# Layer 0's expert lists in four waves instead of five, with the recording planner's ranks drawn anew

## The chip, the core and the metric

The kernel runs on one core of a Trainium2 chip. The metric is device microseconds per execution, the median of several. The kernel before has a median of 1212.02 us over 3 runs (1209.06 to 1213.38). The profiler took one execution by itself; that one is longer, and the text keeps it apart.

## The reference, cut to what matters

Two layers of attention and a mixture of experts, each followed by a residual add and a layer norm, all in float32, on 16 sequences of 256 tokens with 128 features:

```python
x = _layernorm(x + _L0_attn_ref(x, ...))   # RMS norm, 16 heads of 64, softmax over 256 keys
x = _layernorm(x + _L0_ffn_ref(x, ...))    # top 2 of 8 experts (hidden 256) + one shared expert
x = _layernorm(x + _L1_attn_ref(x, ...))   # per token: 16 heads attend to each other, 8 wide
x = _layernorm(x + _L1_ffn_ref(x, ...))    # top 2 of 8 experts (hidden 512)
```

The reference computes every expert for every token and masks; the kernel computes, for most tokens, only the two chosen experts.

## The kernel before, in words

**Groups and units.** The 4096 tokens are eight groups of 512 (`xg[0]` to `xg[7]`), each of four chunks of 128 rows. Layer 0's attention (`attention0`, L666) goes through 128 units, one for a group, a pair of heads and a sequence of 256: scores on PE (TensorE, L574), a maximum on DVE (VectorE, L537), exponentials on ACT (ScalarE, L543), a division on POOL (GpSimd, L558), transposes (L591) and the product with the values (L612) on PE, the latter two three units behind the scores (`LAG`). Sixteen units make a group; then `project` (L629) or `project2` (L649) gives the group's output.

**Lists and waves.** The experts' work is done in waves (`WAVES`, L33). A wave takes some groups; `route` (L799) finds each token's two experts on DVE and gives every pair of token and expert a row in a list that is sorted by expert and padded to tiles of 128 rows. With c chunks in a wave the list has 2c + 7 tiles (`NTS`), enough for any split over eight experts. `send` (L896) copies the tokens' rows into the list in HBM with indirect DMAs that POOL issues, two for each chunk (L905). `lists` (L969) loads the list's rows back, four tiles at a time (L1014), and for each tile the weights of its expert (L1035 and L1039 in layer 0, L1039 and L1048 in layer 1); PE transposes the rows (L1060), does the first products (L1098) and the second ones (L1118), with GELU on ACT between them (L1077, L1071). The results go back to HBM (L1136). `gathered` (L920) fetches them with indirect DMAs from POOL, two for each chunk (L934), and DVE adds them to `x` (L948). `shared` (L1153) is layer 0's shared expert.

**What follows a wave of layer 0.** `middle` (L1397) takes each of its groups through the norm, through layer 1's attention (`attention1`, L1313; `chunk1`, L1201, one for each chunk: products on DVE and POOL at L1216 and L1292, sums on DVE at L1220 and L1267 or on PE at L1226 and L1274) and to the logits of layer 1's router. Layer 1 has three waves of its own, groups 0 to 3, groups 4 and 5, groups 6 and 7; a wave of layer 1 begins when all its groups have their logits (`wave1`, L1411).

**The dense part.** The second sequence of group 7 goes through all experts without lists (`sequence`, L1569, and `dense`, L1502; its products at L1528 and L1541).

**What sets the order.** Nothing is reordered at run time. The kernel's parts are generators ("strands"); while the program is recorded, `everything` (L322) picks the strand to go on with by a small planner: each strand says when its next step can start by the planner's own clocks, `KEYS` gives each kind of strand a rank and a lead in time, `PACE` gives attention0 a lead for each half group, and `COPY`, `SUMS`, `FAVOUR`, `SWITCH` bias which engine a copy or a product goes to. What comes out is one fixed sequence for each engine, and each engine works its own sequence in order and waits at its head. A new value in `WAVES`, `KEYS` or `PACE` therefore moves thousands of instructions without changing what most of them do.

Only one list is open at a time (`held` has "lists"); in layer 1 a list that is not the last can be interrupted by one of layer 0 or by the last one. The names used below: "list 0_3" is layer 0's wave 3, "list 1_0" layer 1's wave 0, and so on.

Of the kernel before, what the change touches and what calls it, by code (L numbers as in the profile page):

```python
# [29 lines left out]


PARTS = [(g, 0, NC) for g in range(LAST)] + [(LAST, 0, NC // 2)]
WAVES = (((0,), (1,), (2, 3), (4, 5), (6, 7)), ((0, 1, 2, 3), (4, 5), (6, 7)))  # L33
I32 = mybir.dt.int32


# [1 line left out]
def two_layers(  # L38
# [81 lines left out]

    CS = [[sum(PARTS[i][2] for i in w) for w in ws] for ws in WAVES]
    NTS = [[2 * c + 7 for c in cs] for cs in CS]
# [14 lines left out]
    def cleared(layer, w):  # L137
# [10 lines left out]

    INF = float("inf")
    KEYS = {  # L150
        "copy qk": (-0.126, 0.098),
        "copy v": (0.258, 0.464),
        "copy p": (0.365, 0.67),
        "copy o": (-2, 0.171),
        "softmax": (-0.332, 0.347),
        "softmax 2": (-0.557, 0.071),
        "summed": (-1.741, 0.444),
        "normalised": (0.126, 0.737),
        "heads": (-0.897, 0.036),
        "w route": (0.203, 0.017),  # L160
        "w send": (-0.299, 0.32),
        "w shared": (-0.925, 0.219),
        "w loads": (-0.335, 0.546),
        "w turns 0": (-0.74, 0.23),
        "w turns 1": (-0.883, 0.07),
        "w firsts 0": (-0.387, 0.019),
        "w firsts 1": (1.618, 0.545),
        "w gelu": (-0.526, 0.095),
        "w seconds 0": (-0.551, 0.301),
        "w seconds 1": (1.137, -0.645),  # L170
        "w stored": (-1.046, -0.735),
        "w gathered 0": (0.929, 0.295),
        "w gathered 1": (0.397, -0.379),
        "w qkv": (-1.874, 0.602),
        "w attention1": (0.552, 0.037),
        "w attention1 2": (0.862, 0.362),
        "w sums": (0.545, 0.099),
        "w normed": (-0.751, 0.178),
        "d loads": (-1.222, 0.561),
        "d route": (0.341, 0.516),  # L180
        "d firsts": (-0.612, -0.163),
        "d gelu": (0.532, 0.418),
        "d seconds": (-0.409, -0.744),
        "d added": (-0.448, 0.337),
        "d normed": (-0.4, 1.013),
    }
    PACE = [-1.37, 1.462, -1.273, -1.636, 1.503, -0.385, -0.54, 1.281]
    PACE += [1.979, 0.872, 0.936, -0.178, 0.47, 1.169, 0.679, 1.086]
    now = [0]
    COPY = -0.06  # L190
    SUMS = 7.789
    FAVOUR = 0.378
    SWITCH, SWITCH_BACK = 0.582, 1.515
    window, unit = [0, 0.0, 1.0], [P]
    clk = {"PE": 0.0, "DVE": 0.0, "ACT": 0.0, "POOL": 0.0, "SP": 0.0}
    table = ["exp"]
# [65 lines left out]
    def copied(o, i, *after):  # L262
# [5 lines left out]
        dve, act = (max(clk[e], *after) + t for e, t in zip(EITHER, us))  # L268
        if dve + COPY <= act:
            nc.vector.tensor_copy(o, i)  # L270
# [37 lines left out]
    def key(what, w=0, i=0):  # L308

        rank, time = KEYS[what]  # L310
        return (time, rank, w, i)
# [5 lines left out]
    def begin(steps, key):  # L317
        st = Strand(steps, key)
        if st.due is not None:
            strands.append(st)  # L320
# [13 lines left out]

    DENSE = len(WAVES[0])
    held = []
# [100 lines left out]
    def after(*names):  # L437

        return lambda: max(end.get(n, INF) for n in names)
# [27 lines left out]
    def normalised(g):  # L467
# [10 lines left out]
        yield at, EITHER  # L478
        if max(clk["DVE"], at) + 1.2 + COPY <= max(clk["ACT"], at) + 1.4:
            for c in range(NC):  # L480
# [16 lines left out]
        hT[g] = sb.tile([P, GT], FP, tag="hT", name=f"hT{g}")  # L497
        if max(clk["DVE"], at) + 0.75 + COPY <= max(clk["ACT"], at) + 0.7:
            nc.vector.tensor_scalar(hT[g], t, nscale_s, None, ALU.mult)
# [6 lines left out]
    def projected(g, p, w, name, to):  # L506

        yield after(("h", g), "wq"), "PE", "m"
        pq = ps_m.tile([P, GT], FP, tag="m", name=f"p{name}{g}_{p}")
        nc.tensor.matmul(pq, w[:, ts(p, P)], hT[g], start=True, stop=True)  # L510
        to[g, p] = sb.tile([P, GT], FP, tag=f"{name}T", name=f"{name}T{g}_{p}")
        begin(copy_out(opened("m"), to[g, p], pq, work("PE", 0.91), name, g, p), key("copy qk"))
# [153 lines left out]
    def attention0():  # L666
        yield from projected(0, 0, wq_s, "q", qT)
        yield from projected(0, 0, wk_s, "k", kT)
        clears = [(0, 0), (0, 1), (0, 2), (1, 0), (0, 3), (1, 1), (0, 4), (1, 2)]
        for u in range(len(UNITS) + LAG):  # L670
            if u >= LAG:
                yield from turn(u - LAG)
            g, p, b = UNITS[u] if u < len(UNITS) else (NG, 0, 0)
            i = u % (2 * NP)
            if g < NG:
                now[0] = 2 * g + i // NP
                running[-1].key = (KEYS["heads"][1], PACE[now[0]], 0, 0)
                if i == 3 and g + 1 < NG:
                    begin(normalised(g + 1), key("normalised"))
                if u + 1 < len(UNITS):  # L680
                    to = UNITS[u + 1]
                    if to[0] == LAST:
                        yield from projected2(*to[1:])
                    elif b:
                        yield from projected(*to[:2], wk_s, "k", kT)
                if g < LAST and b == 0:
                    to = (g, p + 1) if p + 1 < NP else (g + 1, 0)
                    if to[0] < LAST:
                        yield from projected(*to, wq_s, "q", qT)
                if g < LAST:  # L690
                    if i in (3, 5, 7, 9):
                        yield from values(g, 1, (i - 3) // 2)
                elif i in (1, 3):
                    yield from values(g, 1, (i - 1) // 2)
                elif i in (5, 7):
                    yield from values(g, 0, 2 + (i - 5) // 2)
                elif i in (8, 10):
                    yield from values(g, 1, 2 + (i - 8) // 2)
                if i in (11, 13, 15) and g + 1 < LAST:
                    yield from values(g + 1, 0, (i - 11) // 2)  # L700
                if i in (11, 13) and g + 1 == LAST:
                    yield from values(g + 1, 0, (i - 11) // 2)
                if i == 1 and 0 < g < LAST:
                    yield from values(g, 0, 3)
                yield from scores(u)
                if u < 2:
                    for c in (2 * u, 2 * u + 1):
                        yield from values(0, 0, c)
            if u >= LAG:
                yield from attended(u - LAG)  # L710
            if g < NG:
                if u % 3 == 2 and clears and "prepared" in end:
                    cleared(*clears.pop(0))
                if g == LAST and i == NP + LAG:
                    yield from project2(0)
                if g < LAST and i == NP + LAG:
                    yield from project(g, 0)
                if i == LAG and g > 0:
                    yield from project(g - 1, 1)
        yield from project2(1)  # L720
        end["over"] = 0.0
        now[0] = 2 * NG
# [165 lines left out]
    def chunks_of(r):  # L888
        return [(g, c0 + c) for g, c0, n in (PARTS[i] for i in WAVES[r.layer][r.wave]) for c in range(n)]

    def place_of(r, part):

        ws = WAVES[r.layer][r.wave]
        return sum(PARTS[i][2] for i in ws[: ws.index(part)])
# [74 lines left out]
    def lists(r):  # L969
# [3 lines left out]

        yields = layer == 1 and w < len(WAVES[1]) - 1
        if not yields:
# [225 lines left out]
    def chunk1(w, c, o, qv, kv, at, sums):  # L1201
# [5 lines left out]
        for j in range(2):  # L1207
            yield (lambda: max(at, prod_ring.free(), sc_ring.free() if j == 0 else 0.0)), "DVE"
            if j == 0:
                sc1, ks = sc_ring.tile([P, NH1, NH1], "sc")  # L1210
                if "over" in end and clk["PE"] + SUMS < max(clk["DVE"], at) and ends["s"][-2] < clk["PE"] + 1.0:
                    ps = ps_s.tile([P, NH1, NH1], FP, tag="s", name="s1")
# [29 lines left out]
        if place is None:  # L1242
            yield at, ("POOL", "DVE")
            e, us = ("POOL", 0.6) if max(clk["POOL"], at) <= max(clk["DVE"], at) + FAVOUR else ("DVE", 0.4)
            (nc.gpsimd if e == "POOL" else nc.vector).tensor_tensor(
# [39 lines left out]
        for j in range(2):  # L1285
            yield (lambda: max(at, prod_ring.free())), ("POOL", "DVE")
            e, us = "POOL", 2.35
            if max(clk["DVE"], at) + 1.25 + FAVOUR < max(clk["POOL"], at) + 2.35:
                e, us = "DVE", 1.25
# [8 lines left out]
            at2 = work("POOL", us, at, one=us) if e == "POOL" else work("DVE", us, at, ports=True)  # L1298
            if j == 0 and "over" in end and clk["PE"] + SUMS < max(clk["DVE"], at) and ends["s"][-2] < clk["PE"] + 1.0:
                po = ps_s.tile([P, P], FP, tag="s", name="o1_sums")  # L1300
# [65 lines left out]
    def wave(w):  # L1366

        parts, C = WAVES[0][w], CS[0][w]
        yield after("prepared"), None
# [108 lines left out]
    w = DENSE  # L1478
# [185 lines left out]
```

## Time and profile before

| what | value |
|---|---|
| median of 3 runs | 1212.02 us |
| the profiled execution's own time | 1245.39 us |
| its span on the core | 1243.7 us |
| mean granted TensorE clock | 0.943 |
| PE, DVE, ACT, POOL busy | 1109.0, 900.2, 706.0, 705.7 us |
| last `po` of layer 0's attention (L612) begins | 841.4 us |
| first transpose of list 1_0, of list 1_1, of list 1_2 (L1060) | 936, 1075, 1157 us |
| last second product of list 1_2 (L1118) ends | 1211 us |

The page's times are those of the profiled execution. In what follows the stretch up to 841 us is the head and the rest the tail. The five lists of layer 0 stand so in it: sends at 166 to 183, 214 to 227, 451 to 484, 651 to 683 and 839 to 857 us, the last of these at the start of the tail; their gathers at 231 to 242, 281 to 359, 577 to 622, 759 to 822 and 957 to 979 us. Layer 1's three lists are sent at 873 to 923, 1018 to 1038 and 1120 to 1139 us, and gathered from 1084 us to 1233 us.

How to read it: a busy PE alone doesn't say that PE is the bound. What does is a stretch in which PE has no idle time, against one in which it waits at the head of its sequence for another engine.

### The profile page before, as it was taken

What the parts mean: (1) busy time and instruction counts of PE and PEld (TensorE: products, weight loads), DVE (VectorE), ACT (ScalarE), POOL (GpSimd) and SP (SyncE); (2) the same over time, 40 slices, a digit from 0 to 9 for tenths busy, and PEclk for the clock granted to TensorE, in tenths of its full rate; (3) what the DMA queues carried; (4) which work ended last, traced back from release to release, by engine and by line L of the source; (5) the groups of instructions that cost most, each with busy time, mean ns of one, the idle gap of its engine ahead of it and who ended that gap; (6) DMA issues with size and microseconds to landing.
All of it is one profiled execution on the core that took longest, in us unless ns stands there. A gap on an engine that the chain in (4) does not pass through costs nothing.

```text
span 1243.7 us, 22712 instructions
## 1 busy us (share of the span) xinstructions
PE 1109.0 (89%) x7336; PEld 814.5 (65%) x7336; DVE 900.2 (72%) x1811; ACT 706.0 (57%) x2050; POOL 705.7 (57%) x1089
## 2 busy tenths in 40 slices
PE   9999999979999999999998899987838896797883
PEld 5566667665665666766655677655738795697883
DVE  5767675478878888754877998888878795793433
ACT  5556566476665667676674687653544552342432
POOL 4434372557555468524769557767873546446666
PEclk9999999989999999999999999987888897798997
DMA  8900023430000021151003240135458874684952
GB/s 260 270 1 1 1 86 111 132 106 14 1 5 1 1 63 58 35 145 45 18 4 100 80 133 21 29 119 164 144 162 232 257 230 129 197 245 125 288 177 70
DMA packets 187208, 132.47 MB, mean 107 GB/s; under 512 B 12745, under 2 KB 171474, under 8 KB 187090
## 3 DMA queue, kind: packets, MB, share of 16 engines
q1 hardware_dynamic: 179410, 115.27, 31.6%
q0 software_dynamic: 7680, 15.74, 4.1%
q8 instruction: 59, 0.97, 0.3%
q14 instruction: 59, 0.48, 0.1%
HBM read 97.94 MB, written 33.03 MB: 105 GB/s over the span
## 4 chain that ended last, share of the span: by engine, by line
PE 66%; DVE 11%; POOL 8%; issue 6%; ACT 4%; DMA 2%; SPq 1%; ACTq 0%; DVEq 0%; POOLq 0%
PE s L574 9%; PE po L612 9%; PE t L591 9%; PE po_e L1118 6%; PE ph L1098 6%; POOL rows L905 5%; PE py L629 4%; PE pv L528 4%; PE pq L510 4%; PE pk L510 3%; DVE qk_prod L1216 2%; DMA xq<-rows 2%; PE po_d L1541 1%; POOL pr L558 1%; DVE sc L1220 1%
## 5 line engine op out<-in xcount | busy, mean ns | idle before, releaser
L558 POOL TENSOR_SCALAR pr<-pr,rs 128x256 f32<-128x256 f32 x512 | 253.0, 511 | 220.6 <-DVE rs L554 136.7
L543 ACT ACTIVATE pr<-s,nm 128x256 f32<-128x256 f32 x512 | 235.5, 474 | 26.1 <-DVE nm L537 23.0
L537 DVE TENSOR_REDUCE nm<-s 128x4 f32<-128x1024 f32 x128 | 156.1, 1220 | 58.0 <-PE s L574 53.2
L905 POOL DMA_INDIRECT rows<-x,r_pi x120 | 130.7, 1089 | 58.6 <-DVE r_pi L853 24.4
L934 POOL DMA_INDIRECT y<-outs,r_pi x120 | 120.0, 1000 | 65.8 <-issue 27.4
L612 PE MATMUL po<-pT,v 128*64 128x256 f32 x1024 | 146.0, 397 | 7.2 <-ACT h L1077 3.1
L1098 PE MATMUL ph<-xqT,wa 128*128 128x128 f32 x1028 | 132.8, 287 | 16.6 <-issue 14.2
L591 PE MATMUL t<-ident,pr 128*128 128x128 f32 x1024 | 144.4, 283 | 0.8 <-ACT h L1077 0.8
L591 PEld LDWEIGHTS t<-ident,pr 128*128 128x128 f32 x1024 | 115.7, 145 | 42.4 <-POOL pr L558 20.6
L1098 PEld LDWEIGHTS ph<-xqT,wa 128*128 128x128 f32 x1028 | 126.9, 202 | 22.6 <-issue 16.8
L270 DVE COPY pT<-t 128x512 f32<-128x512 f32 x163 | 106.8, 686 | 42.2 <-PE t L591 38.3
L574 PEld LDWEIGHTS s<-kT,qT 64*128 64x128 f32 x896 | 77.1, 186 | 84.2 <-issue 73.1
L574 PE MATMUL s<-kT,qT 64*128 64x256 f32 x896 | 127.0, 402 | 0.0
L1292 POOL TENSOR_TENSOR av_prod<-sc,qkv 128x1024 f32<-128x1024 f32 x35 | 89.9, 2577 | 50.7 <-ACT sc L1254 35.3
L272 ACT COPY oT<-po 128x256 f32<-128x256 f32 x99 | 36.9, 373 | 130.6 <-PE po L612 119.6
L612 PEld LDWEIGHTS po<-pT,v 128*64 128x64 f32 x1024 | 65.1, 137 | 67.6 <-issue 18.9
L543 ACT ACTIVATION_READ_ACCUMULATOR pr<-s,nm 128x1 f32 x512 | 105.5, 206 | 0.0
L1118 PE MATMUL po_e<-wb,h 128*128 128x128 f32 x648 | 84.3, 292 | 5.5 <-issue 5.5
L1118 PEld LDWEIGHTS po_e<-wb,h 128*128 128x128 f32 x648 | 82.6, 209 | 5.3 <-issue 4.8
L1216 DVE TENSOR_TENSOR qk_prod<-qkv 128x1024 f32<-128x1024 f32 x64 | 82.8, 1294 | 1.8 <-ACT qkv L272 1.8
L1267 DVE TENSOR_REDUCE o<-av_prod 128x64 f32<-128x1024 f32 x62 | 73.3, 1200 | 11.3 <-POOL apart L904 9.7
L1220 DVE TENSOR_REDUCE sc<-qk_prod 128x128 f32<-128x1024 f32 x64 | 78.1, 1220 | 2.2
(233 smaller groups left out, 1971.0 us busy)
## 6 DMA issues: line engine op xcount, KB each, us to landing
wa<-in_w_dram SPq DMA_DIRECT2D x190, 128.0 KB
wa<-in_w_dram SPq DMA_DIRECT2D x81, 256.0 KB
wb<-in_w_dram SPq DMA_DIRECT2D x81, 256.0 KB
xq<-rows SPq DMA_DIRECT2D x38, 256.0 KB
outs<-yq SPq DMA_DIRECT2D x38, 256.0 KB
rows<-clear SPq DMA_DIRECT2D x3, 1472.0 KB
rows<-clear SPq DMA_DIRECT2D x1, 2496.0 KB
rows<-clear SPq DMA_DIRECT2D x2, 1216.0 KB
```

Of the source, the lines that this page charges most:

```text
L270: nc.vector.tensor_copy(o, i)
L537: nc.vector.tensor_reduce(nm[u], s, AX.X, ALU.max, negate=True)
L543: nc.scalar.activation(pr[u][:, i, :], s[:, i, :], AF.Exp, bias=nm[u][:, i : i + 1], accum_out=su[u][:, i : i + 1],)
L558: nc.gpsimd.tensor_scalar(pr[u][:, i, :], pr[u][:, i, :], rs[:, i : i + 1], 1.0, ALU.mult, ALU.mult)
L574: nc.tensor.matmul(sc[u][:, j, qc, :], q[part, ts(qc, P)], k[part, :], start=True, stop=True,)
L591: nc.tensor.transpose(t[:, kc, ts(qc, P)], pr[u][:, 2 * j + qc, ts(kc, P)], ident)
L612: nc.tensor.matmul(po[j * DH : (j + 1) * DH, :], vs[g, p // 4, 2 * b + kc][:, ts(h, DH)], pT[u][j][:, kc, :], start=(kc == 0), stop=(kc == 1),
L905: i = nc.gpsimd.indirect_dma_start(out=rows[layer][w][:, :], out_offset=bass.IndirectOffsetOnAxis(ap=r.pos[:, k, c : c + 1], axis=0), in_= ...
L934: nc.gpsimd.indirect_dma_start(out=y, out_offset=None, in_=outs[layer][w][:, :], in_offset=bass.IndirectOffsetOnAxis(ap=r.pos[:, k, c0 + c ...
L1098: nc.tensor.matmul(ph[:, q - q0, c, :], was[i, q][0][:, c, :], xTs[i][0][:, q, :], start=True, stop=True)
L1118: nc.tensor.matmul(po[:, q, :], hs[i, q][0][:, c, :], wbs[i, q][0][:, c, :], start=(c == 0), stop=(c == nh - 1))
L1216: nc.vector.tensor_tensor(m, q3[:, ts(j, HALF)].unsqueeze(2).to_broadcast(full), k3.unsqueeze(1).to_broadcast(full), ALU.mult)
```

## The change

The diff touches constants only. Its core:

```diff
-WAVES = (((0,), (1,), (2, 3), (4, 5), (6, 7)), ((0, 1, 2, 3), (4, 5), (6, 7)))
+WAVES = (((0,), (1, 2), (3, 4), (5, 6, 7)), ((0, 1, 2, 3), (4, 5), (6, 7)))
...
     KEYS = {
-        "copy qk": (-0.126, 0.098),
+        "copy qk": (-0.774, 0.185),
...
-        "w send": (-0.299, 0.32),
+        "w send": (-1.721, 0.333),
...
-    PACE = [-1.37, 1.462, -1.273, -1.636, 1.503, -0.385, -0.54, 1.281]
-    PACE += [1.979, 0.872, 0.936, -0.178, 0.47, 1.169, 0.679, 1.086]
+    PACE = [-1.701, -1.793, -0.961, -1.029, -0.823, 0.7, 1.677, 1.623]
+    PACE += [1.623, 1.362, -1.327, 0.173, 1.701, 2, 1.82, 1.503]
...
-    COPY = -0.06
-    SUMS = 7.789
-    FAVOUR = 0.378
-    SWITCH, SWITCH_BACK = 0.582, 1.515
+    COPY = 0.617
+    SUMS = 7.519
+    FAVOUR = 0.528
+    SWITCH, SWITCH_BACK = 1.21, 0.864
...
-        clears = [(0, 0), (0, 1), (0, 2), (1, 0), (0, 3), (1, 1), (0, 4), (1, 2)]
+        clears = [(0, 0), (0, 1), (0, 2), (1, 0), (0, 3), (1, 1), (1, 2)]
```

All 35 entries of `KEYS` have new values. With c = 4, 4, 8, 8, 6 chunks the lists of layer 0 had 15, 15, 23, 23 and 19 tiles, 95 in all; with c = 4, 8, 8, 10 they have 15, 23, 23 and 27, 88 in all. Group 5, which was in a wave with group 4, is now in the last one, with 6 and the first sequence of 7. One of the clears of the lists' memory goes.

Both programs can be built and their sequences compared without being run. Counts of instructions, and where they stand in each engine's sequence, are taken from there below.

## The prediction

> **What bounds the kernel now.** I read first the page's 40 slices and then the busy time by stage, cut at the points where PE's sequence passes from one kind of work to the next.
>
> ```profile
> PE   9999999979999999999998899987838896797883
> PEclk9999999989999999999999999987888897798997
> ```
>
> The first line is PE's busy tenths, the second the granted clock. But for slice 9 and slices 22 and 23, PE is full up to slice 26; behind it there are holes, and the clock sinks with them.
>
> ```profile
> core 0: us, PE busy (x) PEld busy (x) DVE busy (x) ACT busy (x) POOL busy (x), PEclk, DMA share, GB/s
> 0.00:841.00 841.00, 806.28 (x5176) 535.05 (x5176) 632.40 (x1210) 539.28 (x1727) 470.13 (x792) 0.98 0.23 68
> 841.00:936.00 95.00, 61.30 (x359) 50.00 (x359) 76.88 (x139) 42.10 (x98) 70.48 (x100) 0.81 0.53 163
> 936.00:1075.00 139.00, 110.06 (x814) 104.59 (x813) 107.29 (x196) 59.63 (x102) 66.09 (x74) 0.84 0.74 218
> 1075.00:1157.00 82.00, 71.66 (x522) 67.64 (x521) 51.29 (x136) 34.30 (x61) 43.89 (x55) 0.90 0.60 177
> 1157.00:1211.00 54.00, 47.18 (x376) 45.36 (x377) 19.69 (x80) 21.57 (x42) 35.50 (x42) 0.97 0.81 233
> 1211.00:1244.00 33.00, 12.49 (x97) 11.89 (x96) 12.66 (x55) 9.08 (x20) 19.64 (x29) 0.76 0.23 67
> ```
>
> The head is bound by PE: 806 of 841 us. The tail is not: in 403 us PE works 303. I call its stages A (to the first transpose of list 1_0), B (to that of 1_1), C (to that of 1_2), D (to the last second product) and E. In A, DVE and POOL are busier than PE. What PE waits for in A is in the timeline of PE:
>
> ```profile
> 917.00 0.38 PE L419 MATMUL t_x<-ident,o 128*128 128x128 f32 x2
> 932.58 0.69 PE L419 MATMUL t_x<-ident,o 128*128 128x128 f32 x2 [15.20 <-DVE o L1308]
> ```
>
> A transpose of layer 1's attention output stood 15.2 us at the head of PE's sequence, until DVE had finished the chunk; everything behind it stood too.
>
> **The change, part by part.** I take each instruction's time up to the start of the next on its engine, from the trace; so taken, a first product costs 0.247 us, a second 0.243, a list transpose 0.14. A tile of layer 0 (one transpose, two of each product) costs PE 1.1 us.
>
> *Seven tiles and one routing less.* 7 x 1.1 = 8 us of PE; but 16 more sums go to PE (L1226, 0.33 each, as L1274), 5 us. PE's total is nearly unchanged. Seven tiles also save 14 GELUs and 7 pairs of weight loads; one route saves about 40 short DVE instructions, scan included, some 10 us. These lie beside PE work in the head. So the tiles themselves are worth little; what counts is where the work goes.
>
> *The head gets shorter.* Its lists were 15 + 15 + 23 + 23 = 76 tiles, and are 15 + 23 + 23 = 61. Up to the last L612, PE has 30 first products, 30 second ones and 15 transposes less, 17 us; and of the shared expert, routing and layer 1's attention of one group and a half some 11.5 us less: 28.5 us. The head's PE idle time is 35 us: 11 of it lie at 205 to 300, where two waves' sends and gathers kept POOL from the divisions of L558, 8 at 650 to 705, in the sends of wave (4, 5). The new order has one wave less, but puts sends in one block: 16 in a row before unit 55's and unit 89's divisions. At the timeline's pitch of 1.27 us for a send (0.96, a memset, the gap) a block is 20 us; three units of `LAG` at 5 us (the scores of units 103 and 105 are 10 us apart) cover 15, and PE's order has 6 us of shared-expert products in the hole. Bounds: 0 to 20 us of hole for a block; the nearest row, the 16 sends at 651 to 683, cost 8. I take the idle time as unchanged, 35 us. The head ends at 841.4 - 28.5 = 813.
>
> *Copies.* `COPY` sends 104 copies more to ACT and 109 fewer to DVE. ACT's 539 us in the head rise by about 98 x 0.5 less the GELUs saved, to some 565 of 813; DVE falls by 70. PE still covers both; an exponential that waits behind one copy in ACT's sequence loses at most 0.59 us (a copy of `pT`). Bounds -10 to +10 us, taken at nothing.
>
> *The tail gets 25 us more PE work* (296 us to 321 by the same counting): 8 tiles, the shared expert for three parts, one more group of layer 1's attention, the sums. By stage, before and after: A 55.8 and 92.5; B 105.5 and 134.1; C 71.9 and 54.5; D 49.0 and 39.9; E 13.8 and 0. The dense experts' products, which lay in C, D and E, now lie in A and B (19 and 32 us). POOL's work behind its last division goes from 240 to 270 us (8 sends and 8 gathers more), DVE's behind its last maximum from 283 to 268.
>
> Stage A. List 1_0 can't start before its rows are sent. DVE passed 34.7 us of work from its last maximum (826) to the list positions (873), 47 us, 0.74; up to group 4's `y` (87.7 us, 937) it was 0.79. In the new order 56.4 us stand before those positions, because group 3's attention now ends in the tail: 74 us at 0.76, so 59 us after the head's end. Then 32 sends x 1.27 = 41, and about 10 for the rows' load: A = 110 (95 before). POOL has finished the 20 sends of 0_3 before. PE's own 92.5 fit, if it stands no more than 17 us; group 4's transpose, the one shown, comes at 65.5 us of DVE work, at about 70 us, and 35 us of PE work follow it.
>
> Stage B. List 1_0 itself: 101 us of PE plus 20 of standing (29 in B before, 10.9 in one wait for a weight load): 121. Now the sends of 1_1 stand on POOL behind six gathers of 1_0, which wait for all of 1_0's results: 3 + 6 gathers and the products between them, 9, + 16 sends, 20, + 9 for the load = 41. Dense products, 33 us, cover PE for most of it. B = 162 (139 before). 1_1's positions are due at 186.4 us of DVE work, about 225 us behind the head, and 1_0's end at 231: just hidden.
>
> Stages C, D, E. At before's ratios: 54.5 x 82/71.9 = 62; 39.9 x 54/49.0 = 44; E, the last gathers and norms on POOL and DVE, stays 33, since the dense products that go from it lay beside them. POOL has the sends of 1_2 done some 49 us of work behind those of 1_1, inside C.
>
> Sum: 813 + 110 + 162 + 62 + 44 + 33 = 1224 us of span. The profiled execution's time is 1.7 us over its span: 1225.7 against 1245.4, 0.984. Applied to the median: 1212 x 0.984 = 1193.
>
> *A rule that speaks against it.* The Trainium skill, "TensorE: Matmul & The Clock Gate", Part 1, says that PE drops to half clock after an idle window of about 3.4 us. The change moves 25 us of PE work from a head at clock 0.98 to a tail at 0.81 to 0.90. By the rule at its worst they cost 50, and the forecast 1217, slower. The trace: the 304 records of second products in the head took 37.27 us, 0.123 each; in B 312 took 41.86, 0.134, in D 152 took 18.25, 0.120. Products come in bursts that are warm; I take the row, at most 9% or 2 us, which the stages' ratios contain.
>
> **Rivals.** (1) *Stage A keeps its ratio.* PE's fixed sequence stands behind DVE: A took 95 us for 55.8 of PE work, 1.70; with 92.5 that is 157. In the new order the transposes and sums of groups 3 and 4 (L419, L1274) stand ahead of list 0_3 and in it, so each wait holds list 0_3, then the gathers, then group 5's attention and list 1_1. For it: the 15.2 us above. Against: DVE has less ahead of those points (65.5 us to group 4's, not 87.7). Span 1271, time 1239, slower by 2.2%. It decides from A = 130 on: there the span is as before.
> (2) *The blocks of sends tear holes in the head*: 20 us each instead of 8, twice: +16 to 20, time 1208 to 1212, no change. For: POOL can't do a division in 20 us. Against: PE's order has shared products there.
> (3) *Less standing in the tail*: the 10.9 us weight wait goes, A is 104, the head loses 5 us of holes as it has a wave less: 1224 - 22 = 1202, time 1171. For: DVE has 80 us less in the head and 15 in the tail.
> (4) That nothing moves: excluded, since the sequences differ everywhere; but head and tail can cancel, as in (2).
>
> **How the numbers follow.** Forecast 0.40, (1) 0.25, (2) 0.15, (3) 0.20. Around each case lie 10 us. A measurement of this kernel can tell about 0.3% from no change. Faster: 0.34 of the forecast, all of (3), a fourth of (2): 0.58. Within 0.3%: 0.12. Slower: nearly all of (1), a part of (2) and a little of the forecast: 0.30. The range goes from (3) to short of (1)'s full size: 1168 to 1234.
>
> **What would show it.** Last L612 at 813 (over 828: rival 2, with PE holes at units 55 to 60 and 89 to 94); first transpose of 1_0 110 us later (over 130: rival 1, with DVE named at L419 or L1274); of 1_1 at 162 more, with POOL's sends behind L934; E still 33 us. I am wrong if list 0_3 waits for its own sends or weights, or if the copies on ACT hold up the exponentials.

## The result and the profile after

The changed kernel takes 1240.13 us (median of 4 runs, 1237.33 to 1240.6), the kernel before 1212.13 beside it: ratio 1.0227, 95% interval 1.0208 to 1.0247. It is slower, by 28 us, where 19 us less had been forecast.

One thing has to be known to read the numbers: in some sessions (runs made together on one chip) nearly all runs of the kernel before lie within 10 us of 1212 us and in others of 1247, so each kernel is set against the kernel before of its own session; I call them sessions of 1212 and of 1247, and this result is from one of 1212.

The page's two lines for PE and its granted clock, of the changed kernel:

```profile
PE   9999999999899999989899999977989889679491
PEclk9999899999999999999899999996999989879695
```

But for three slices at 8, PE is again full up to slice 26, and the holes behind it are again where lists follow each other. The busy time by stage, cut at the same points of PE's sequence (last L612; first transposes of lists 1_0, 1_1, 1_2; last second product):

```profile
core 0: us, PE busy (x) PEld busy (x) DVE busy (x) ACT busy (x) POOL busy (x), PEclk, DMA share, GB/s
0.00:819.00 819.00, 787.76 (x4980) 516.21 (x4981) 573.13 (x1046) 563.97 (x1780) 450.14 (x763) 0.97 0.21 61
819.00:932.00 113.00, 95.13 (x608) 82.57 (x606) 64.78 (x157) 47.83 (x120) 73.06 (x118) 0.84 0.61 185
932.00:1091.00 159.00, 131.08 (x960) 121.01 (x958) 139.18 (x244) 79.66 (x139) 102.40 (x103) 0.92 0.62 185
1091.00:1167.00 76.00, 53.76 (x434) 52.88 (x435) 36.63 (x125) 30.35 (x57) 49.22 (x64) 0.84 0.81 237
1167.00:1211.00 44.00, 40.63 (x323) 39.83 (x323) 12.88 (x54) 19.06 (x37) 22.02 (x26) 0.90 0.76 221
1211.00:1238.00 27.00, 0.00 (x0) 0.00 (x0) 6.12 (x26) 2.75 (x7) 13.94 (x18) 0.55 0.18 51
```

The head is 819 us, PE's work in the stages behind it 95.1, 131.1, 53.8, 40.6 and 0, almost as counted (92.5, 134.1, 54.5, 39.9, 0). The stage that is out of line is C: 76 us for 53.8 of work. PE's timeline says where they go:

```profile
1091.23 1.97 PE L1060 MATMUL px<-ident,xq 128*128 128x128 f32 x8 [4.75 <-DMA xq<-rows]
...
1146.34 2.84 PE L1118 MATMUL po_e<-wb,h 128*128 128x128 f32 x24
1166.89 1.09 PE L1060 MATMUL px<-ident,xq 128*128 128x128 f32 x4 [17.71 <-DMA xq<-rows]
```

List 1_1 has ended at 1149 and PE stands 17.71 us until the first rows of list 1_2 are loaded. The longest waits of PE in the whole tail, in us, times, longest:

```profile
PE px L1060 <- DMA xq<-rows: 22.9, 3, 17.7
PE s L1226 <- DVE qk_prod L1216: 9.1, 1, 9.1
PE o_sums L1274 <- DVE av_prod L1292: 8.7, 1, 8.7
PE t_x L419 <- DVE o L1308: 6.1, 2, 3.9
```

The wait for the attention's output at L419, 15.2 us at once before, has gone to 6.1 in two; the largest now is one for rows.

### The profile page after: what moved, and what is told of

It reads as the page before. It is cut to its first block, busy times and chain, and to the rows that moved or that the text cites. A ratio compares the mean times of both kernels' runs of the same rounds, so it can differ in the third digit from the quotient of the medians.

```text
span 1238.3 us, 22483 instructions
## 1 busy us (share of the span) xinstructions
PE 1108.4 (90%) x7299; PEld 812.5 (66%) x7299; DVE 832.7 (67%) x1648; ACT 743.6 (60%) x2139; POOL 710.8 (57%) x1090
## 4 chain that ended last, share of the span: by engine, by line
PE 60%; DVE 17%; POOL 10%; issue 4%; DMA 4%; ACT 4%; SPq 0%; ACTq 0%; DVEq 0%; POOLq 0%
PE s L574 10%; PE po L612 9%; PE t L591 9%; POOL rows L905 6%; PE ph L1098 4%; PE pv L528 4%; PE po_e L1118 4%; PE pk L510 4%; PE py L629 3%; PE pq L510 3%; DVE qk_prod L1216 3%; DMA y<-outs,r_pi 3%; DVE o L1267 2%; DVE sc L1220 2%; ACT pr L543 2%
## 5 line engine op out<-in xcount | busy, mean ns | idle before, releaser
L612 PE MATMUL po<-pT,v 128*64 128x256 f32 x1024 | 143.9, 396 | 4.8 <-DVE pT L270 3.4
L905 POOL DMA_INDIRECT rows<-x,r_pi x120 | 125.8, 1048 | 36.6 <-issue 21.3
L1098 PE MATMUL ph<-xqT,wa 128*128 128x128 f32 x1000 | 130.2, 288 | 5.5 <-ACT h L1071 3.7
L1098 PEld LDWEIGHTS ph<-xqT,wa 128*128 128x128 f32 x1000 | 124.7, 203 | 10.2 <-ACT h L1071 4.3
L1292 POOL TENSOR_TENSOR av_prod<-sc,qkv 128x1024 f32<-128x1024 f32 x40 | 100.7, 2525 | 33.4 <-DVE o L1267 13.5
L272 ACT COPY oT<-po 128x256 f32<-128x256 f32 x110 | 41.4, 376 | 113.1 <-PE po L612 113.1
L612 PEld LDWEIGHTS po<-pT,v 128*64 128x64 f32 x1024 | 63.9, 137 | 66.0 <-issue 11.7
L270 DVE COPY pT<-t 128x512 f32<-128x512 f32 x124 | 81.8, 687 | 37.4 <-PE t L591 37.3
L948 DVE SCALAR_TENSOR_TENSOR x<-y,r_gate,x 128x128 f32<-128x128 f32 x120 | 47.5, 400 | 81.6 <-DMA y<-outs,r_pi 80.4
L272 ACT COPY pT<-t 128x512 f32<-128x512 f32 x132 | 74.3, 593 | 39.9 <-PE t L591 39.6
L1216 DVE TENSOR_TENSOR qk_prod<-qkv 128x1024 f32<-128x1024 f32 x64 | 94.8, 1482 | 3.4 <-ACT qkv L272 3.3
L1220 DVE TENSOR_REDUCE sc<-qk_prod 128x128 f32<-128x1024 f32 x62 | 75.6, 1220 | 2.1
L1118 PE MATMUL po_e<-wb,h 128*128 128x128 f32 x648 | 77.0, 278 | 0.0
```

The costliest lines, as they stand in the source:

```text
L272: nc.scalar.copy(o, i)
L612: nc.tensor.matmul(po[j * DH : (j + 1) * DH, :], vs[g, p // 4, 2 * b + kc][:, ts(h, DH)], pT[u][j][:, kc, :], start=(kc == 0), stop=(kc == 1),
L905: i = nc.gpsimd.indirect_dma_start(out=rows[layer][w][:, :], out_offset=bass.IndirectOffsetOnAxis(ap=r.pos[:, k, c : c + 1], axis=0), in_= ...
L1098: nc.tensor.matmul(ph[:, q - q0, c, :], was[i, q][0][:, c, :], xTs[i][0][:, q, :], start=True, stop=True)
L1118: nc.tensor.matmul(po[:, q, :], hs[i, q][0][:, c, :], wbs[i, q][0][:, c, :], start=(c == 0), stop=(c == nh - 1))
L1216: nc.vector.tensor_tensor(m, q3[:, ts(j, HALF)].unsqueeze(2).to_broadcast(full), k3.unsqueeze(1).to_broadcast(full), ALU.mult)
```

## The experiments

I began with two theories. First, on the base: the recorded execution of before (the one that was profiled ahead of the prediction) took 1245.39 us where its other runs took 1212, and my sum was made against it. If it carried 31 us that belong to that execution alone, the ratio 0.984 was drawn on a wrong base. Second, on the tail: the new waves cost more behind the head than they save in it; either because the ranks don't fit, or because of the waves.

### 1. The kernel before once more, and each half of the change alone

The first is the kernel before, unchanged; the second has the new `WAVES` (and the one clear less) with the old `KEYS`, `PACE` and constants; the third the reverse.

```diff
-WAVES = (((0,), (1,), (2, 3), (4, 5), (6, 7)), ((0, 1, 2, 3), (4, 5), (6, 7)))
+WAVES = (((0,), (1, 2), (3, 4), (5, 6, 7)), ((0, 1, 2, 3), (4, 5), (6, 7)))
```

> The kernel before, unchanged, profiled once more. Theory 1: the profiled execution of before (1245.4 us) was not like its others (1209 to 1213), and the factor 0.973 that the prediction carried over to the new kernel belongs to that one execution. Then the span here is about 1210 us, and the 31 us are missing in waits that the first trace had, most of them in the tail (the weight waits of 10.9 us at 1030 and of the stretch from 1124). Theory 2: being profiled costs this kernel some 33 us and the new one nothing. Then the span here is about 1244 us again.

> Four waves with the ranks of before. Theory W (the partition costs: 20 sends, 27 tiles and three groups' attention begin only behind the head): 1235 us or more. Theory R (the partition is good, the new ranks are bad for it): below 1215 us. Since the old ranks were chosen for five waves, a time above 1240 alone does not tell W from a misfit; the stages of its profile do: W wants the last list to be late in it too.

> Five waves with the new ranks, paces and biases. Theory W: 1210 to 1220 us, as before, since the partition is that of before. Theory R: 1235 us or more.

A session of 1212. Before again: 1213.71 us (12 runs), ratio 1.0001 (0.9986 to 1.0016), and its profiled execution took 1213.84. So a profile does not cost 31 us. By stage:

```profile
0.00:842.00 842.00, 807.58 (x5179) 536.75 (x5180) 632.73 (x1219) 540.09 (x1727) 469.84 (x796) 0.98 0.23 68
842.00:934.00 92.00, 58.18 (x352) 49.04 (x351) 73.98 (x129) 42.07 (x98) 68.53 (x96) 0.80 0.53 165
934.00:1060.00 126.00, 102.66 (x814) 97.49 (x814) 108.76 (x196) 59.21 (x102) 65.84 (x74) 0.91 0.81 242
1060.00:1132.00 72.00, 68.30 (x529) 65.29 (x529) 50.77 (x132) 34.40 (x61) 40.78 (x53) 0.94 0.67 200
1132.00:1177.00 45.00, 43.73 (x371) 42.69 (x370) 19.98 (x80) 21.86 (x42) 34.70 (x41) 1.00 0.94 276
1177.00:1212.00 35.00, 13.16 (x101) 12.37 (x99) 13.36 (x57) 8.85 (x20) 22.66 (x32) 0.75 0.23 70
```

Against the recorded profile (head 841, then 95, 139, 82, 54, 33) the head is the same within 1 us, and B, C and D are 13, 10 and 9 us shorter, with C and D nearly full of PE work. One stretch shows what the recorded execution had: the main block of list 1_1's sends. First the recorded profile of before, then this run:

```profile
1021.00:1039.00 18.00, 7.89 (x64) 7.16 (x62) 13.80 (x18) 1.38 (x4) 15.34 (x27) 0.84 0.70 217
```

```profile
1016.00:1034.00 18.00, 17.57 (x154) 17.11 (x153) 17.76 (x27) 9.58 (x17) 15.32 (x27) 1.00 0.73 220
```

POOL works as long in both (15.3 us); PE did 64 products against 154, and ACT 4 instructions against 17. Ten microseconds of B are here.

What PE waited for in them is in the list of its waits. Where the profile shows nothing that an engine waited for, it says "issue" (or "remote"). The two largest such entries in the tail of the recorded profile, then the only one in that of this run:

```profile
PE ph L1098 <- issue: 14.2, 5, 10.9
PE po_e L1118 <- issue: 6.3, 5, 3.0
```

```profile
PE ph L1098 <- issue: 0.4, 1, 0.4
```

All such entries together are 31 us in the tail of the recorded execution (4, 16, 5 and 6 in A to D) and 0.4 in this one. In sum they are as large as what it took longer, though not stage by stage.

The waves alone took 1289.53 us, 1.0626 times before (1.0588 to 1.0665); the ranks alone 1347.25, 1.1089 (1.1034 to 1.1143). Neither half works by itself: with the old ranks A grows to 160 us, and with the new ranks on five waves list 1_0's sends slip into the head, where they keep POOL from the divisions. The waits of PE between 700 and 1040 us of that run begin with

```profile
PE t L591 <- POOL pr L558: 34.4, 2, 20.9
```

This is the mechanism of rival 2, at a block of 32 sends. But what the waves cost and what the ranks cost can't be told apart by crossing them.

### 2. Where the tail's time is: PE's work, or lists that come late

Theory P: the 35 us of PE work that the tail has more are themselves the cost. Theory L: group 5, which now leaves layer 0 in its last wave, makes list 1_1's rows late, and 1_2's behind them. In the changed kernel (1) and in before (2) layer 1's dense experts are left out, and with them their share in the last half group's output; (3) has another partition in layer 1; (4) moves the gathers back in rank. Of (1) and (2) one of the edited lines is shown.

```diff
-                    for c in range(2):
+                    for c in range(2 if layer == 0 else 0):
...
-WAVES = (..., ((0, 1, 2, 3), (4, 5), (6, 7)))
+WAVES = (..., ((0, 1, 2, 3), (4,), (5, 6, 7)))
...
-        "w gathered 1": (1.684, -0.54),
+        "w gathered 1": (1.684, -20),
```

> The changed kernel without layer 1's dense experts: their first and second products (L1528, L1541), GELUs (L1514) and additions are left out, so the last half group lacks those experts' share in its output; every other instruction stays in its place. That takes some 32 us of PE work out of stage B of the tail. Theory P (what the tail has more of PE work is itself the cost): the time falls by 25 to 33 us, to 1207 to 1215. Theory L (list 1_1's rows come too late, and 1_2's behind them, so that PE waits there whatever it has to do): the products lie under that wait, the time falls by less than 8 us, and the first transpose of list 1_1 shows a wait of 20 us or more.

> The kernel before with the same left out (layer 1's dense experts, 32 us of PE work, which lie in stages C, D and E there; the last half group lacks those experts' share in its output). Theory P: PE bounds C and D, 18 of the 32 us come off, time 1190 to 1196; the 13.8 us in E lie beside the last gathers and norms and come off for nothing. Theory L says nothing else of this kernel, but if the tail's end is set by gathers and norms that start from the last list, the fall is the part of C and D alone, 10 to 20 us.

> The changed kernel with one other partition of layer 1: lists of groups 0 to 3, 4 alone, and 5 to 7 with the first half, in place of 0 to 3, 4 and 5, 6 and 7. As many tiles; the head is the same; list 1_1 no longer waits for group 5, which left layer 0 in the last wave. Theory L: 1_1's rows come some 30 us earlier and 1225 or less. Theory P: the PE work is the same, so 1240 within 5 us.

> The changed kernel with the due time of layer 1's gathers put 20 later in the rank (KEYS w gathered 1: -20 for -0.54): the sends of list 1_1 come ahead of all gathers of 1_0 on POOL, and routing and sends of 1_2 ahead of the combines of all but the first half group. Theory L: the 17.7 us that PE stands at the first transpose of 1_2 go, B ends 5 to 10 us earlier, 1217 to 1228; part of it may come back in E, where more gathers stand behind the last list. Theory P: 1240 within 5 us.

It was a session of 1247 (before 1249.11 over 23 runs), which I had not reckoned with. In the order above: 1321.09 us (1.0577), 1245.69 (0.9965, 0.9948 to 0.9981), 1355.41 (1.0840), 1360.78 (1.0890). All variants of the changed kernel were far above the 1240 that it had taken, so the three were run again, beside the changed kernel itself. Before without the dense experts has a head of 843 us, then 93 and 140 for A and B: the marks of the recorded execution (841, 95, 139), and not those of the session of 1212 (842, 92, 126).

> The changed kernel as it is, beside the same three variants, as the measure for them: in the four runs before this one the kernel before took 1249 us on its chip and not 1212[...]. If that belongs to the chip, then on a chip where before takes 1212 this kernel takes 1240 within 4 us, and on one where before takes 1249 it takes 1340 or more. If it belongs to the edits of the variants, it takes 1.023 times before on either chip.

> As in the earlier run of this edit (layer 1's dense experts left out, 32 us of PE work in stages A and B; the last half group lacks those experts' share in its output), now read against the changed kernel on the same chip. Theory P (the added PE work of the tail is the cost): 25 to 33 us below the changed kernel. Theory L (list 1_1's rows are late and PE waits there): less than 8 us below.

> As in the earlier run of this edit (layer 1's lists of groups 0 to 3, 4 alone, 5 to 7; as many tiles, the head the same), read against the changed kernel on the same chip. Theory L: list 1_1's rows no longer wait for group 5, and 10 to 20 us come off, unless 1_2, now 20 tiles instead of 12 and last, gives them back in D and E: there its gathers and norms stand behind it. Theory P: within 5 us of the changed kernel.

> As in the earlier run of this edit (layer 1's gathers put 20 later in the rank), read against the changed kernel on the same chip. Theory L: the 17.7 us at the first transpose of 1_2 go and B ends earlier; 12 to 20 us below the changed kernel, of which E may take back up to 10. Theory P: within 5 us of it.

Again a session of 1247 (before 1248.32). The changed kernel took 1326.69 us, 1.0629 (1.0579 to 1.0680): what was slow belonged to the session, not to the edits. Against it, without the dense experts 1321.65, with the other partition 1356.51, with late gathers 1358.69.

- Theory P fell here: 32 us of PE work out of the tail, all of it in B, gave 5 us back in the changed kernel, and 3.4 in before, where it lies in C, D and (13 of the 32) in E. In a session of 1212 it was not tested.
- Theory L got its mechanism but not its gain. With group 5 in the last list, B is 127 us instead of 166; but C is 114 instead of 93, D 83 instead of 44 and E 40 instead of 28, as the last list now has 20 sends and 20 gathers instead of 12, and they stand at the end. The gain is given back, and the time is 30 us longer.
- The late gathers were a poor edit: they also moved the last groups' logits behind list 1_1 in PE's sequence, so that 1_2 was sent from 1236 instead of 1210 us. They say nothing on L.

### 3. Why the changed kernel takes 87 us more in a session of 1247

Same program, same orders, spans 1238.3 and 1319.0. Set beside each other, the two traces part in jumps. In the head each lies in a block of sends: PE is behind by 6 us after those of list 0_0, 21 after 0_1's, 26 after 0_2's (between them it makes up a few); in A it goes from 27 to 58 in those of 1_0. That block, first in the session of 1212, then in that of 1247:

```profile
880.00:922.00 42.00, 38.25 (x296) 36.47 (x295) 18.73 (x49) 19.31 (x60) 35.60 (x64) 0.96 0.78 240
```

```profile
907.00:949.00 42.00, 15.43 (x105) 13.96 (x104) 10.83 (x23) 6.78 (x23) 35.63 (x64) 0.70 0.33 105
```

POOL sends at the same pitch in both (1.31 us on average); the other engines get a third to a half of their instructions out. In the second one's timelines of ACT and of PE:

```profile
920.49 0.59 ACT L272 COPY yq<-po_e 128x512 f32<-128x512 f32 x1 [5.57 <-remote]
948.78 1.14 ACT L1077 ACTIVATE h<-ph,r_bias 128x128 f32<-128x128 f32 x4 [27.70 <-remote]
```

```profile
937.48 0.37 PE L1118 MATMUL po_e<-wa,h 128*128 128x128 f32 x1 [1.73 <-issue]
939.61 0.37 PE L1118 MATMUL po_e<-wa,h 128*128 128x128 f32 x1 [1.75 <-issue]
949.97 1.22 PE L1098 MATMUL ph<-xqT,wa 128*128 128x128 f32 x4 [9.99 <-issue]
```

These are waits of the same kind as in the recorded execution; ACT starts again when the block ends (948). They are the mark of the session: over the whole execution PE's waits on "issue" come to 16 to 60 us in the ten profiles from sessions of 1247 with all sends in place (one of them is that of before without the dense experts, the one with 16), to 0 to 3 in the seven from sessions of 1212, and to 31 in the recorded one.

Theory S: in such a session a send holds up what the other engines issue. To test it, every second send was replaced by POOL work of like length, orders unchanged, in both kernels; half of the rows then stay zero. With them ran a kernel in which list 1_2 reads the rows of 1_1 (so the last groups' output is that of other rows), so that it need not wait for its own, and the one without dense experts.

```diff
                 yield r.at, "POOL"
-
+                if k == 1: [nc.gpsimd.memset(clear, 0.0) for _ in range(4)]; at = work("POOL", 1.25, r.at); continue
...
-                    in_=rows[layer][w][t0 * P : (t0 + n) * P, :].rearrange("(t p) d -> p t d", p=P),
+                    in_=rows[layer][1 if (layer, w) == (1, 2) else w][t0 * P : (t0 + n) * P, :].rearrange("(t p) d -> p t d", p=P),
```

> The changed kernel with every second send (L905, the second expert's row of each token) replaced by four memsets on POOL of about the same length together; half of the rows stay zero, so the output lacks the second expert's share; all orders stay as they are. Theory S (a send holds up the instruction streams of the other engines on the chips where before takes 1248): on such a chip half of the 23 us that the head has more than on the quicker chip go, and half of what stands in A and later, so the time falls from 1327 by 25 to 45 us, to 1282 to 1302. If something else of that chip is slow, it stays within 8 us of 1327. On a chip where before takes 1212: 1240 within 6 us by either.

> The kernel before with the same replacement of every second send. Theory S: on a chip where before takes 1248, half of its 35 us go, 1225 to 1237; that is less than in the changed kernel, whose sends stand in longer blocks. If the sends are not it: 1248 within 5 us. On a chip where before takes 1212: 1212 within 5 us by either.

> The changed kernel with list 1_2 reading the rows of list 1_1 instead of its own, so that its loads no longer wait for its own sends (the output of the last groups is that of other rows); the weights it loads still wait for its routing, and all orders stay as they are. Theory L (the late rows of 1_2 are a cost by themselves): the 17.7 us at its first transpose shrink to a few, and the time falls by 10 to 17 us. Theory P, or if the weights come as late as the rows: less than 5 us.

> The changed kernel without layer 1's dense experts once more (32 us of PE work of stages A and B left out, and with it those experts' share in the last half group's output), wanted on a chip where before takes 1212. Theory P: 25 to 33 us below 1.023 times before. Theory L: less than 8 below. On a chip where before takes 1248 it took 1.059 times before, 5 us below the changed kernel, and should again.

A session of 1247 (before 1244.96, 23 runs). The changed kernel with half its sends took 1248.97 us, 1.0026 (1.0001 to 1.0052): 6% of before's time gone, more than I had expected of theory S. Before with half its sends took 1213.48, 0.9753 (0.9687 to 0.9820). Both come to what they take whole in a session of 1212, within 9 and 2 us; that it is so near is in part chance, since the stages differ (A of before is 81 us, where it is 92 there, and D 56, where it is 45). The block of list 1_0, sends and memsets in turn:

```profile
875.00:909.00 34.00, 31.84 (x261) 30.63 (x261) 15.19 (x36) 19.78 (x61) 28.55 (x91) 1.00 0.71 214
```

PE is full in it, and of the 46 us that PE waited on "issue" over the whole execution 9 are left (in before with half its sends 3). Theory S stands: the sends are what holds up the others. The head of this run ends at 813 us.

The kernel with the rows of 1_1 took 1316.72, 1.0586 (1.0511 to 1.0660), and the one without dense experts 1319.18, 1.0599. The former is not clearly below the changed kernel's 1.0629, and its trace says why: PE still waits 14.7 us at 1_2's first transpose, for loads that stand in SP's sequence in order with others that need the list's routing. So it is not the sends alone that are late there; the routing is.

### 4. Set apart, the sends cost their own length

Is it the number of sends, or that they stand back to back? All sends stay, with four or two memsets (0.21 us each by their records, which overlap) after each; the edit with four is shown:

```diff
-                nc.gpsimd.memset(apart, 0.0)
+                nc.gpsimd.memset(apart, 0.0); [nc.gpsimd.memset(clear, 0.0) for _ in range(4)]
```

> The changed kernel with all its sends, and four memsets on POOL (0.84 us together) after each, so that their pitch is some 2.2 us; orders as they are, output whole. POOL has 120 x 0.9 = 108 us more, of which some 29 (32 sends of list 1_0) lie on the path in stage A, and 14 to 18 in each block of sends in the head, part of it in holes. If what holds up the other engines is that sends stand back to back: on a chip where the changed kernel takes 1327, the 80 us go and some 30 to 60 come back: 1275 to 1310. If it is their number: 1327 plus 29 or more, 1350 and up.

> The same with two memsets (0.42 us) after each send, pitch some 1.75 us: POOL has 54 us more, 14 on the path in stage A. Back to back, with a threshold between 1.27 and 1.75: 1260 to 1290 where the changed kernel takes 1327; if the hold-up falls only in proportion to the pitch: about 1300 to 1320; if it is the number of sends: 1340 and up.

> The kernel before with two memsets after each send, output whole. On a chip where it takes 1245 to 1249, some 33 us are the sends' hold-up; 14 come back in stage A. Back to back: 1222 to 1240, faster than both kernels on that chip; by the number of sends: 1255 to 1270. On a chip where before takes 1212 there is nothing to gain, and it takes 1215 to 1235.

This was a session of 1212 (before 1213.72), so that question stayed open. What they show instead is what POOL's time in the sends is worth where nothing is held up: 1341.33 us with four (1.1041, 1.1006 to 1.1075), 1283.31 with two (1.0576, 1.0550 to 1.0602), and before with two 1244.29 (1.0250, 1.0225 to 1.0276), 9 us above what I had allowed for. In a row, the sends' pitch goes from 1.26 us to 1.64 with two memsets and to 2.17 with four, 0.38 and 0.91 more for a send.

| stage, us | before | with two memsets | after | with two | with four |
|---|---|---|---|---|---|
| head | 842 | 850 | 819 | 834 | 850 |
| A | 92 | 104 | 113 | 132 | 162 |
| B | 126 | 134 | 159 | 166 | 173 |
| C | 72 | 73 | 76 | 76 | 81 |
| D + E | 80 | 84 | 71 | 74 | 74 |
| span | 1212.1 | 1244.7 | 1238.3 | 1281.7 | 1339.8 |

In the changed kernel 120 sends with 0.38 us more each are 46 us of POOL's time, and 43 of them come out in the span; in before 33. In the changed kernel's A stand 52 sends (20 and 47 us more): 19 and 49 us longer. In its B the 16 of list 1_1 (6 and 15 us): 7 and 14 longer. In its head 40 sends (15 us with two): 15 longer, where before has 48 (18 us): 8 longer. A and B of the changed kernel end by POOL's sends, nearly one for one, and its blocks in the head lie almost bare.

## Why the prediction was wrong

**Head: 813 forecast, 819 measured.** PE's work fell by 19.8 us against the ordinary before (the execution of experiment 1), not by 28.5, and the holes shrank from 34 to 31. Rival 2's holes did not show in size (its own sum, 16 to 20 us for two blocks at 20 instead of 8, should have been 24), but the slope of experiment 4 says that they are at the edge: what a block grows by, the head grows by.

**Stage A: 110 forecast, 113 measured.** The chain was right up to its last link: the sends of 1_0 begin 61 us behind the head (59 forecast) and last 41.5 (41). The list starts 10 us later, as forecast, but that is luck: PE doesn't stand for the rows. It stands for a norm: POOL works at it (L381) only behind the sends, ACT follows (L409), and the transpose of its result is ahead of the list in PE's sequence. First the changed kernel, then the same with two memsets behind each send:

```profile
923.81 1.63 PE L419 MATMUL t_x<-ident,x 128*128 128x128 f32 x4 [3.39 <-ACT x L409]
```

```profile
957.81 1.63 PE L419 MATMUL t_x<-ident,x 128*128 128x128 f32 x4 [15.80 <-ACT x L409]
```

Rival 1 would have needed 130, and did not occur. In a session of 1247 A was 146, but by the hold-up (26 us of PE's waits in it are on "issue"), not by DVE.

**Stage B: 162 forecast, 159 measured**, by another road, so that the nearness is luck. I had the sends of 1_1 behind the gathers of 1_0. They came when their positions did: at 1062 us, 243 behind the head where I had 225, when list 1_0 had been over for 20 us. "Just hidden" was wrong; layer 1's dense products, which all lie in B (the 19 us of A are layer 0's), filled PE meanwhile up to 1069. In the ordinary before the positions of 1_1 were there at 1012, 24 us ahead of 1_0's end, and B cost 126.

**Stage C: 62 forecast, 76 measured: the term of the sum that was mis-sized.** I had the sends of 1_2 "inside C", as hidden. But list 1_1 ended at 1149, and 1_2's routing had only just been done. DVE's timeline:

```profile
1128.62 0.42 DVE L813 TENSOR_TENSOR_SCAN r_scratch<-going,both 128x128 f32<-128x128 f32 x1
1128.96 1.36 DVE L948 SCALAR_TENSOR_TENSOR x<-y,r_gate,x 128x128 f32<-128x128 f32 x4
...
1138.44 0.35 DVE L948 SCALAR_TENSOR_TENSOR x<-y,r_gate,x 128x128 f32<-128x128 f32 x1 [1.08 <-DMA y<-outs,r_pi]
1140.86 0.21 DVE L829 TENSOR_TENSOR r_scratch<-r_scratch,count 128x48 f32<-128x48 f32 x1 [2.06 <-ACT r_scratch L272]
...
1143.11 0.17 DVE L853 CAST r_pi<-r_pos 128x12 int32<-128x12 f32 x1
```

The last groups' logits are there only at 1120, and the routing's scan (L813) at 1128. Then DVE works off ten combines of list 1_0 (L948), six of which wait for their gathers, 5.1 us in all. But they are not the last to end: the routing's next step (L829) waits 2.06 us more, for sums that come from PE by ACT, and PE came to these only at 1139, behind list 1_1's products and a wait of its own:

```profile
1139.32 0.42 PE L817 MATMUL pc<-both,earlier 128*128 128x48 f32 x2 [2.00 <-ACT yq L272]
```

Then 12 sends to 1159; SP has 17 loads of the list's weights, which need its routing too, ahead of the rows' in its sequence (1145 to 1161) and comes to these at 1162; the rows are there at 1167, 17.7 us after PE ran out of work. In the ordinary before 1_2 was sent from 1107 to 1123, inside list 1_1 (1060 to 1132). That B was full and its lists late, I had seen; that the lateness goes on into C, not.

**D and E: 44 and 33 forecast, 44 and 27 measured.** POOL's work in E is 13.9 us, where the ordinary before has 22.7. That the dense products have gone from E is not the reason: before without them has an E of 37 us (33 in the recorded one). Why POOL has less there is not shown.

**PE's work.** "PE's total is nearly unchanged" was wrong by 15 us: 1093.6 in the ordinary before, 1108.4 now. (The recorded before has 1109.0, but its products take longer beside the waits on "issue"; the changed kernel in a session of 1247 has 1128.) The tail has 320.6 (321 forecast), but the ordinary before had 286 there, not 296. Of the 35 us more, 14 are the lists' (L1060, L1098, L1118: 194.6 to 208.5), 8 the sums of L1226, 7 the shared expert's. And 13 us of dense products that lay in E now lie in B. Of the 25 us that the half clock weighed in the prediction would have cost, the rows show at most 7, over all first products: their records in the tail went from 0.1225 us each (88.7 us for 724) to 0.1315 (99.4 for 756), 7%, where I had taken 2 us in all; those of second products stayed at 0.12.

**The sum and the base: the step that failed.** The span forecast was 1224, measured 1238.3: 14 us, which is C's term. The other 33 of the 47 us came in one line: "Applied to the median: 1212 x 0.984 = 1193". It took for granted that the recorded execution was the kernel, 2.7% stretched. It was not stretched: its head was the same as in the ordinary run, and its 31 us stood behind it, nearly all in B, C and D, together with as many us of PE's waits on "issue", 10 us of its length in one block of sends. By its time, its stage marks and these waits it was of the kind of the sessions of 1247. The largest of the waits, 10.9 us, I had seen and called "one wait for a weight load"; the profile names nothing that it waited for. The head and A were built from chains of POOL, DVE and PE work that hardly contain such waits, so the sum was near what a session of 1212 gives; and then I took 2.7% off it for a stretch that was not in it. Set against 1212.1, the ordinary span of before, the same 1224 would have said 1% slower. C and D I had scaled by the recorded stages' ratios, which do contain such waits; by the ordinary ones they would have been 57 and 41, the sum 1216, no change, and C's term short by 19 us and not by 14.

In a session of 1247, where the base was at home, the changed kernel took 1.063: there the sum was wrong by 95 us of span, as its blocks of sends held up what no block of before had: 31 us in list 1_0's alone.

**What remains open.** Between the two profiled executions, 1212.1 and 1238.3, the tail has 49 us more and the head 23 less. That A and B end by sends and what comes behind them rather than by PE's work is shown, in a session of 1212 by the slopes and for B, in those of 1247, by the dense experts left out. How the 49 divide between group 5's place and the ranks is not: the one kernel that moved group 5 gave its gain back in C to E.

## What to carry to other kernels

Before a sum made on a profile is scaled to a median, ask whether the profiled execution is an ordinary one: here it was 2.7% above the others, and the excess lay in three stages and not in all. The profile alone could have warned: 31 us of PE's waits in it are on "issue", where an ordinary execution has 0.4. Take differences stage by stage from an execution whose time is that of the median. And when waves are merged, count the sends that stand in one block: in the changed kernel what was added to their time on POOL came out at the end nearly one for one (43 of 46 us), in the kernel before at seven tenths (33).

## What the runs showed that was not expected

In the sessions of 1247, a block of 32 indirect sends on POOL (0.96 us each, pitch 1.27) left PE 15.4 of 42 us of work where it otherwise had 38.3, with waits that the profile puts down to issue; ACT stood 27.7 us at once, and PE and SP got an instruction out about every 2.1 us in parts of it. With half as many sends, at a pitch of 2.17 us, 9 us of PE's 46 us of such waits were left, and 78 us were gone from the changed kernel's time and 31 from that of the one before.

The number of sends alone does not decide. In a session of 1247 the head of before (the kernel without layer 1's dense experts, which all lie in the tail) has 48 sends, with divisions between them, at mean pitches of 1.8 to 2.4 us in its four blocks, and ends where it does in a session of 1212 (842.8 and 842.0 us); the changed kernel's has 40 at 1.28 to 1.39 and ends 23 us later (842.1 against 819.2). That points to spacing; but what stands between the sends differs too, and no run changed the spacing alone in such a session. What the engines share with the sends is not known. A late load of instructions is not seen: the trace's two instruction queues bring none between 911 and 956 us, and ACT starts again at 948. Nor is it shown to be a property of one chip: chip 2, on which before took 1244.96 us in the third of these sessions, gave 1213.72 in the next.
